# The end of a two-layer metaformer kernel: half-size PSUM tiles, wider bias passes, output biases on another engine, more repeated products

## The chip, the cores and the metric

The kernel runs on one core of a Trainium2 chip. A core has TensorE (PE; its weight loads are listed as PEld), VectorE (DVE), ScalarE (ACT), GpSimd (POOL) and SyncE (SP, which here issues most transfers), and 16 DMA engines that all queues share. Matrix products are written to PSUM, 128 partitions by eight banks of 512 fp32 values. The metric is the device time of one execution, the median of several runs, in microseconds (us). All data are fp32; each matrix product appears in the trace as two records.

## The reference

The input x is 16 samples of 128 channels by 32 x 32 positions (1024 tokens). Layer 0 adds linear attention and then a spectral convolution over the tokens. Layer 1 adds a residual block of two 3x3 convolutions to the normalised x, and then this mixture of 64 experts:

```python
def _L1_ffn_ref(x, gate_w, gate_b, weight1, weight2):
    logits = jnp.einsum('bsd,ed->bse', x, gate_w) + gate_b
    probs = jax.nn.softmax(logits, axis=1)            # over the 1024 tokens
    vals, idx = jax.lax.top_k(probs.transpose(0, 2, 1), K)    # K = 8
    ...
    pooled = jnp.einsum('bked,bke->bed', gathered, topv)
    h = jnp.concatenate([pooled.transpose(1, 0, 2), ones], axis=-1)
    h = jax.nn.gelu(jnp.einsum('ebd,edh->ebh', h, weight1), approximate=False)
    h = jnp.concatenate([h, ones], axis=-1)
    out = jnp.einsum('ebh,eho->ebo', h, weight2)
    out = out.transpose(1, 0, 2)
    weighted = jnp.einsum('beo,bke->bkeo', out, topv).reshape(Bn, K * E, O)
    outputs = jnp.zeros((Bn, Sn, O), dtype=x.dtype)
    outputs = outputs.at[jnp.arange(Bn)[:, None], flat_idx].add(weighted)
    return outputs
```

`x` here is the layer norm of each token over its channels. `weight1` has 129 rows of 512 per expert (the last is a bias), `weight2` 513 rows of 128 (the last is a bias). Each expert picks 8 tokens of a sample, pools them with their softmax weights, runs one small network on the pooled vector, and adds its output to the same tokens with the same weights.

## The kernel before

The change touches the end of layer 1. What comes ahead of it (layer 0, up to about 630 us) is unchanged.

**The convolution stage** takes the 16 samples one after another, overlapped. Every sample is a list of some fifty operations (`table`); a planner, given a duration and a due time for each, writes the order in which all engines issue them, and a few operations of the last samples are then moved by hand (`move`). The order is fixed: each engine executes its own instructions in that order. An operation is a method of `Routed`; sample 14 uses the subclass `Other`, sample 15, the last, uses `Final`. The last sample's part after its convolutions is, in this order:

- `last`: per half of the positions, DVE adds the residual and updates x, PE transposes four 128x128 blocks to tokens (`flip`), DVE takes statistics of the blocks (`count`);
- `stats2`, `root2`, `scales2`: the second half's statistics, then the scale and the shift of each token;
- `norm2`: four blocks are normalised on DVE and four on ACT;
- `channels`: PE transposes the tokens back, half by half, into `pu`, and DVE and ACT copy one half each into `tk`;
- `logits`: PE multiplies `tk` of samples 14 and 15 by the gate weights. `Final` does it twice, into two tiles, so that DVE (`replace`) and ACT (`exp`) have one each;
- `largest`: DVE finds the eight largest of each row (MAX8 on each half, then on the two results) and the bias of the exponential; `exp`: ACT, with the row sum; `replace`: DVE marks the eight largest (MATCH_REPLACE8);
- `gates`: DVE keeps the marked exponentials, PE transposes them, ACT and DVE copy one half each to `gtt`;
- `pool`, `pool_copy`, `pooled`, `pooled_copy`: PE pools the tokens by the gates, DVE scales, PE transposes, DVE copies to `pooled`.

PSUM has three one-bank slots (tag `cv`), two two-bank slots (tag `big`) and one more (tag `s`). A tile of tag `big` holds both halves of a sample. A tile that takes a slot over waits until the former tile's readers are done. `keep` issues products of the identity with itself into a tile of tag `cv`; nothing reads them.

**The experts** follow. They are taken in 16 groups of four. Group g: `hidden(g)` adds four products to biases that stand in PSUM already, and ACT applies GELU; `turn` transposes that (copied by DVE); `output` multiplies by the second weights (copied by DVE); `collect` transposes the result into `ot`. The loop runs them staggered: in iteration g PE issues `turn` of g-1, `hidden` of g, `collect` of g-2 and `output` of g-1. `biases(g)` writes the hidden biases of a pair of groups: for each of four experts and of two groups one product of a broadcast column of the identity (32 rows) with 32 rows of `b1`, into a 32-row strip of the group's PSUM bank. It runs before the loop for groups 0 and 1, into two `cv` slots, and in the loop at every even g, into a `big` slot.

The expert weights come as 32 pieces ("halves") of 1 MB. The first 15 are loaded before the loop; each later one is issued by SP when the product that used its place is done (`freed`), and after the weights ten loads of parked samples (`xb`). Once the expert outputs stand in `ob` (DVE: output times the sample's factor `rs`, plus the output bias, which ACT put there beforehand, L1951), the last stage (L1989) multiplies them by the gates of all samples, and DVE, or ACT with POOL, adds the products to x, which SP writes out, 512 KB a sample.

**Beside this**, at the head of the convolution stage (about 626 to 668 us) SP issues, in program order, the loads of samples 0 and 1, of the convolution weights `cw`, of `b1` (two loads) and of the output biases `b2` (two loads), and then those of samples 2 and up (x from `xd`, and `y` from `yd`).

Of the kernel before, what the change touches and what calls it, by code (L numbers as in the profile page):

```python
# [8 lines left out]
F32 = mybir.dt.float32  # L9
# [5 lines left out]
P = 128  # L15
# [54 lines left out]
def metaformer_kernel(ctx: ExitStack, tc: tile.TileContext, io: dict, out: bass.AP):  # L70
# [1029 lines left out]
    b1 = gpool.tile([E, HID], F32, name="b1")  # L1100
# [4 lines left out]
    with ExitStack() as c1:  # L1105
# [114 lines left out]
        idle = {(13, "turn"): 4, (13, "pooled"): 2, (15, "logits"): 2, (15, "turn"): 1}  # L1220
# [368 lines left out]

        class Other(Routed):  # L1590
# [12 lines left out]
        class Final(Routed):  # L1603
# [11 lines left out]
            def count(self, h):  # L1615
                for j in range(4 * h, 4 * h + 4, 2):
                    nc.vector.bn_stats(
                        self.bst[:, j : j + 2, :].rearrange("p j s -> p (j s)"),
                        self.pt[:, j : j + 2, :].rearrange("p j c -> p c j"),
                    )  # L1620

            def flip(self, dst, src, h):
                for j in range(4):
                    nc.tensor.transpose(dst[:, j, :], src[:, 4 * h + j], ident)

            def last(self):
                v = nc.vector
                self.pt = tokens(big())
                xj = self.x.rearrange("p (j c) -> p j c", c=P)
                for h in range(2):  # L1630
# [11 lines left out]
                    self.flip(self.pt[:, 4 * h : 4 * h + 4], xj, h)  # L1642
# [6 lines left out]
            def norm2(self, i):  # L1649
# [3 lines left out]
                r, nm = self.sts[:, 0, :], self.sts[:, 3, :]  # L1653
                for j in range(4):
                    nc.vector.tensor_scalar(
                        self.tt[:, j], self.pt[:, j], r[:, j : j + 1], nm[:, j : j + 1],
                        ALU.mult, ALU.add,
                    )
                normalize(self.tt, self.pt, r, nm, 4, NT)
# [8 lines left out]
            def logits(self):  # L1668
                super().logits()
                one = self.pl  # L1670
                super().logits()
                self.pl, self.pl2 = one, self.pl

            def exp(self):
                one, self.pl = self.pl, self.pl2
                super().exp()
                self.pl = one

            def largest(self):
                v = nc.vector  # L1680
                self.top = work.tile([P, TOPK], F32, name="top", tag="top")
                two = work.tile([P, 2 * TOPK], F32, name="two", tag="two", bufs=1)
                for h in range(2):
                    v.max(two[:, h * TOPK : (h + 1) * TOPK], self.pl[:, halves2[h]])
                v.max(self.top, two)
                self.ss = work.tile([P, 3], F32, name="sm", tag="sm")
                v.tensor_tensor(self.ss[:, 0:1], self.top[:, 0:1], gb, ALU.add)
                v.tensor_tensor(self.ss[:, 1:2], gb, self.ss[:, 0:1], ALU.subtract)

            def gates(self):  # L1690
                self.pg = tokens(big())
                self.gtt = work.tile([P, NT, P], F32, name="gtt", tag="tok", bufs=1)
                gj = self.gt.rearrange("p (j c) -> p j c", c=P)
                for h, copy in enumerate((nc.scalar.copy, nc.vector.tensor_copy)):
                    cs, js = halves2[h], slice(4 * h, 4 * h + 4)
# [3 lines left out]
                    self.flip(self.pg[:, js], gj, h)  # L1699
                    copy(self.gtt[:, js], self.pg[:, js])  # L1700
                nc.vector.reciprocal(rs[:, self.pr : self.pr + 1], self.ss[:, 2:3])
# [108 lines left out]

        def biases(g):

            for i in range(EG):
                for r in range(2):
                    rows = slice(r * E // 2, (r + 1) * E // 2)
                    at = r * E // 2 + g // 2 * EG + i
                    nc.tensor.matmul(
                        phs[g + r][i * CG : (i + 1) * CG, :],
                        ident[rows, at : at + 1].to_broadcast([E // 2, CG]), b1[rows, :],
                        start=True, stop=False, skip_group_check=True,  # L1820
                    )
# [22 lines left out]
        with tc.manual_schedule(engines=PINNED | {mybir.EngineType.SP}):  # L1844
# [4 lines left out]
            bs = w1[:, C, :].rearrange("(k r i) h -> r k i h", r=2, i=EG)  # L1849
            for r in range(2):  # L1850
                nc.sync.dma_start(b1[r * E // 2 : (r + 1) * E // 2, :], bs[r])
# [4 lines left out]
            for b, name in order:  # L1856
# [15 lines left out]
                if b == B - 1 and name == "logits":  # L1872
                    for g in range(2):
                        phs[g] = ps.tile([P, HID], F32, name="ph", tag="cv", bufs=3)
                    biases(0)
# [19 lines left out]
        def hidden(g):  # L1895
            w1t = halves[2 * g]
            if g % 2 == 0:
                if g:
# [262 lines left out]
```

## Time and profile before

| | us |
|---|---|
| median of 3 runs (lowest to highest) | 1220.72 (1220.01 to 1222.14) |
| the profiled execution's own time | 1224.1 |
| its span, first to last instruction | 1222.0 |
| busy: PE / DVE / ACT / POOL | 1145.7 / 943.2 / 727.2 / 604.7 |
| mean granted TensorE clock, share of full speed | 0.981 |
| first transposes of the last sample's tokens | 1112.75 |
| pooling of the last pair starts | 1130.08 |
| first products of the first expert group | 1133.24 |
| first final product | 1191.16 |
| first output issued | 1195.90 |

A line of the order of time gives start, duration, engine, source line, operation, written tile <- read tiles, shapes and count; the brackets hold how long the engine had stood idle and what ended that wait. A line of the stretches gives, for each engine, the busy time and the number of instructions, then the granted PE clock, the busy share of the DMA engines (it can read a few per cent over 1) and their rate. SPq lines are issues of transfers, and their time is that of issuing.

### The profile page before, as it was taken

Reading aid. Unit: us, or ns where it says so; the run is one execution under the profiler, and the core shown is the slowest. Engines: PE = TensorE matmul, PEld = TensorE weight load, DVE = VectorE, ACT = ScalarE, POOL = GpSimd, SP = SyncE. Lnnn points to the kernel's source line nnn. Section 1 sums busy time; section 2 is a strip of 40 time slices with the busy share of each in tenths; the row PEclk is TensorE's granted clock in tenths of the full one; section 3 lists DMA queues with packets and bytes.
Section 4 is the critical chain, followed back from the end, with each engine's and each line's share of the span. In section 5 each row is a group of like instructions: output and inputs, shape, how many; then the busy total and the mean of one; then the engine's idle time right before and its main releaser. Section 6 shows DMA issues by size and latency. Waiting matters only on the chain.

```text
span 1222.0 us, 34375 instructions
## 1 busy us (share of the span) xinstructions
PE 1145.7 (94%) x14322; PEld 941.2 (77%) x14322; DVE 943.2 (77%) x1953; ACT 727.2 (60%) x1447; POOL 604.7 (49%) x806
## 2 busy tenths in 40 slices
PE   6899999999998999999997899999999999998995
PEld 5667767787767999999996788888888888885452
DVE  6999999878655777777764689898888989877335
ACT  6777776878564777777752345555555555554211
POOL 2786436454557688888872434343333333231003
PEclk8999999999998999999998999999999999999997
DMA  7224463322234334444458311233233321416997
GB/s 285 87 91 173 159 208 117 104 87 86 71 123 146 97 134 142 141 135 140 141 175 265 99 52 53 86 103 120 80 119 116 104 87 70 173 35 238 369 408 312
DMA packets 91546, 175.13 MB, mean 143 GB/s; under 512 B 6016, under 2 KB 42112, under 8 KB 90752
## 3 DMA queue, kind: packets, MB, share of 16 engines
q1 hardware_dynamic: 88672, 168.95, 41.3%
q0 software_dynamic: 640, 2.49, 0.7%
q8 instruction: 112, 1.84, 0.6%
q10 hardware_dynamic: 2080, 1.51, 0.4%
q14 instruction: 42, 0.34, 0.1%
HBM read 110.28 MB, written 62.65 MB: 142 GB/s over the span
## 4 chain that ended last, share of the span: by engine, by line
PE 47%; DVE 27%; issue 11%; ACT 5%; DMA 5%; POOL 4%; SPq 0%; POOLq 0%; DVEq 0%; ACTq 0%
PE pcv L1211 10%; PE pg L987 9%; PE py L1011 9%; DVE bst L135 4%; PE big L573 3%; PE big L152 3%; PE big L172 3%; PE big L643 3%; DVE abss L1454 1%; DVE xp L1476 1%; PE big L534 1%; DVE xp L1338 1%; PE big L451 1%; DVE sts L128 1%; ACT tt L144 1%
## 5 line engine op out<-in xcount | busy, mean ns | idle before, releaser
L1211 PE MATMUL pcv<-v,cw 128*128 128x256 f32 x1152 | 259.9, 382 | 4.1 <-POOL v L1401 4.1
L1211 PEld LDWEIGHTS pcv<-v,cw 128*128 128x128 f32 x1152 | 215.9, 191 | 37.7 <-issue 4.9
L998 DVE COPY g<-pg 128x512 f32<-128x512 f32 x196 | 127.8, 683 | 70.6 <-PE pg L987 70.6
L1000 ACT COPY g<-pg 128x512 f32<-128x512 f32 x316 | 161.2, 606 | 30.1 <-PE pg L987 29.4
L987 PE MATMUL pg<-ph,mst 32*128 32x128 f32 x4096 | 139.3, 280 | 1.6 <-DVE x L650 0.9
L987 PEld LDWEIGHTS pg<-ph,mst 32*128 32x128 f32 x4096 | 126.5, 188 | 15.7 <-DVE g L998 8.2
L1011 PE MATMUL py<-g,v 128*32 128x128 f32 x4096 | 126.2, 276 | 4.3 <-POOL v L978 2.6
L1011 PEld LDWEIGHTS py<-g,v 128*32 128x32 f32 x4096 | 109.0, 111 | 12.5 <-POOL v L978 2.8
L144 ACT ACTIVATE tok<-tok,sts 128x128 f32<-128x128 f32 x256 | 101.9, 481 | 15.9 <-DVE sts L1288 13.6
L978 POOL TENSOR_TENSOR v<-xc 128x256 f32<-128x256 f32 x128 | 97.5, 785 | 15.8 <-DMA xc<-vd 15.5
L135 DVE BATCH_NORM_STATS2 bst<-big 128x6 f32<-128x256 f32 x252 | 89.6, 417 | 17.4 <-PE big L152 11.6
L643 PE MATMUL big<-u,mu 128*128 128x128 f32 (+4 forms) x384 | 86.2, 381 | 0.1
L1401 POOL TENSOR_TENSOR v<-abss 128x256 f32<-128x256 f32 x64 | 49.1, 787 | 68.1 <-DVE abss L1397 56.7
L1420 POOL TENSOR_TENSOR yo<-abss 128x256 f32<-128x256 f32 x32 | 23.5, 733 | 109.9 <-DVE abss L1416 109.9
L643 PEld LDWEIGHTS big<-u,mu 128*128 128x128 f32 x384 | 57.3, 191 | 23.8 <-issue 15.8
L573 PE MATMUL big<-wf,ub 128*128 128x256 f32 x256 | 65.1, 391 | 3.6 <-ACT ub L144 1.5
L476 POOL TENSOR_TENSOR ke<-ke,ks 128x1024 f32<-128x1024 f32 x16 | 30.6, 1915 | 72.4 <-DVE qs L484 42.7
L979 POOL TENSOR_SCALAR v<-v 128x256 f32<-128x256 f32 x64 | 55.2, 862 | 5.6
L573 PEld LDWEIGHTS big<-wf,ub 128*128 128x128 f32 x256 | 45.8, 192 | 15.4 <-ACT ub L144 7.9
L287 POOL TENSOR_TENSOR xf<-ab 128x256 f32<-128x256 f32 x34 | 25.2, 741 | 64.4 <-DVE ab L254 64.3
L144 ACT ACTIVATE tt<-tt,sts 128x128 f32<-128x128 f32 x120 | 47.8, 481 | 14.8 <-DVE sts L1288 13.1
L144 ACT ACTIVATE ub<-ub,sts 128x128 f32<-128x128 f32 x128 | 50.8, 479 | 8.9 <-DVE sts L566 8.9
(284 smaller groups left out, 2460.1 us busy)
## 6 DMA issues: line engine op xcount, KB each, us to landing
we<-in_weight SPq DMA_DIRECT2D x31, 1024.0 KB, 10.4
xc<-vd SPq DMA_DIRECT2D x64, 256.0 KB, 3.0
yd<-ys SPq DMA_DIRECT2D x32, 512.0 KB, 3.6
vd<-xf SPq DMA_DIRECT2D x15, 1024.0 KB, 5.1
y<-yd SPq DMA_DIRECT2D x15, 896.0 KB, 6.1
x<-in_x SPq DMA_DIRECT2D x16, 512.0 KB, 4.8
mi<-in_M_phi SPq DMA_DIRECT2D x16, 512.0 KB, 4.5
xd<-x SPq DMA_DIRECT2D x15, 512.0 KB, 3.0
```

The costliest lines, as they stand in the source:

```text
L135: nc.vector.bn_stats(bst[:, j : j + 2, :].rearrange("p j s -> p (j s)"), src[:, j : j + 2, :].rearrange("p j c -> p c j"),)
L144: nc.scalar.activation(dst[:, j, :], src[:, j, :], AF.Identity, bias=nm[:, j : j + 1], scale=r[:, j : j + 1],)
L573: nc.tensor.matmul(dst, self.ub[:, q, :], wf[:, q, :], start=True, stop=True)
L643: nc.tensor.matmul(self.pa[:, a:hi], mu[:, NF - 1 - si, tap, :], self.u[:, a - tap : hi - tap], start=(tap == 0), stop=(tap == KU - 1),)
L978: nc.gpsimd.tensor_tensor(vv[:, x, 1:, bs], e, o, op)
L979: nc.gpsimd.tensor_scalar(v[:, :, 0, bs], v[:, :, 2, bs], -1.0, None, ALU.mult)
L987: nc.tensor.matmul(pg[r][:, i], mst[rs, 4 * q + i, :], ph[rs, c, :], start=True, stop=True,)
L998: nc.vector.tensor_copy(dst, src)
L1000: nc.scalar.copy(dst, src)
L1011: nc.tensor.matmul(py[rows, x, kl, :], v[:, (x * NM + m) * JL + jl, 1 - ri : 3 - ri, :] .rearrange("p k b -> p (k b)"), g[:, ((x * 2 + ri) ...
L1211: nc.tensor.matmul(pc[:, i], wt[:, dy, k, :], v[:, k, dy * WT : dy * WT + HT], start=(dy == 0), stop=(dy == 2),)
L1401: nc.gpsimd.tensor_tensor(v[:, k, WT : WT + HT], self.ab[:, 0], self.ab[:, 1], op)
```

## The change

It does the following:

- In the last sample every two-bank tile of the tokens, of one set of logits and of the transposed gates becomes two one-bank tiles (`quarter()`, tag `cv`). The order of normalisation in `norm2` is turned round: ACT's half is issued first.
- One of the two sets of logits is computed half by half; each half's MAX8 follows its products, the exponential reads these halves in two instructions with a sum each, and a DVE addition joins the sums. `replace` reads the other set.
- In `gates` both gate products and transposes are issued before the two copies.
- `biases` does four groups in a pass: `b1` takes 128 partitions (16 rows of each 32 hold biases; a POOL memset clears the rest), is loaded in four pieces, and a pass has 16 products on 32x32 tiles of the array, into four banks. The first pass moves from behind `logits` to behind `gates`; the others run at g = 4, 8 and 12.
- The output biases move from ACT, ahead of the loop, to DVE inside it, one pair per iteration from g = 3 to 10.
- `keep` gets two more products after the logits, one less after the gates, and one in each of four places at the end of the expert stage.

```diff
-    b1 = gpool.tile([E, HID], F32, name="b1")
+    b1 = gpool.tile([P, HID], F32, name="b1")
+    nc.gpsimd.memset(b1, 0.0)
...
-        idle = {(13, "turn"): 4, (13, "pooled"): 2, (15, "logits"): 2, (15, "turn"): 1}
+        idle = {(13, "turn"): 4, (13, "pooled"): 2, (15, "logits"): 4}
...
+        def quarter():
+            return ps.tile([P, 4, P], F32, name="pq", tag="cv", bufs=3)
...
             def last(self):
                 v = nc.vector
-                self.pt = tokens(big())
+                self.half = []
...
                     if h:
                         self.count(0)
-                    self.flip(self.pt[:, 4 * h : 4 * h + 4], xj, h)
+                    self.half.append(quarter())
+                    self.flip(self.half[h], xj, h)
...
+                normalize(self.tt[:, 4:], self.half[1], r[:, 4:], nm[:, 4:], 0, 4)
                 for j in range(4):
                     nc.vector.tensor_scalar(
-                        self.tt[:, j], self.pt[:, j], r[:, j : j + 1], nm[:, j : j + 1],
+                        self.tt[:, j], self.half[0][:, j], r[:, j : j + 1], nm[:, j : j + 1],
                         ALU.mult, ALU.add,
                     )
-                normalize(self.tt, self.pt, r, nm, 4, NT)
...
             def logits(self):
+                self.two = work.tile([P, 2 * TOPK], F32, name="two", tag="two", bufs=1)
+                self.lg = []
+                for h in range(2):
+                    pl = quarter()
+                    self.lg.append(pl.rearrange("p j c -> p (j c)"))
+                    for jj in range(2):
+                        nc.tensor.matmul(
+                            self.lg[h][jj * E : (jj + 1) * E, :], gw,
+                            tks[self.b - 1 + jj][:, halves2[h]],
+                            start=True, stop=True, skip_group_check=True,
+                        )
+                    nc.vector.max(self.two[:, h * TOPK : (h + 1) * TOPK], self.lg[h])
                 super().logits()
-                one = self.pl
-                super().logits()
-                self.pl, self.pl2 = one, self.pl
...
+            def exp(self):
+                self.gt = work.tile([P, N], F32, name="eg", tag="eg", bufs=1)
+                for h in range(2):
+                    nc.scalar.activation(
+                        self.gt[:, halves2[h]], self.lg[h], AF.Exp, bias=self.ss[:, 1:2],
+                        accum_out=self.ss[:, 2 + h : 3 + h],
+                    )
...
-                for h, copy in enumerate((nc.scalar.copy, nc.vector.tensor_copy)):
-                    cs, js = halves2[h], slice(4 * h, 4 * h + 4)
+                pg = []
+                for h in range(2):
+                    cs = halves2[h]
                     nc.vector.scalar_tensor_tensor(
                         self.gt[:, cs], self.lr[:, cs], LOW, self.gt[:, cs], ALU.is_le, ALU.mult
                     )
-                    self.flip(self.pg[:, js], gj, h)
-                    copy(self.gtt[:, js], self.pg[:, js])
-                nc.vector.reciprocal(rs[:, self.pr : self.pr + 1], self.ss[:, 2:3])
+                    pg.append(quarter())
+                    self.flip(pg[h], gj, h)
+                for h, copy in enumerate((nc.scalar.copy, nc.vector.tensor_copy)):
+                    copy(self.gtt[:, 4 * h : 4 * h + 4], pg[h])
+                total = self.ss[:, 2:3]
+                nc.vector.tensor_tensor(total, total, self.ss[:, 3:4], ALU.add)
+                nc.vector.reciprocal(rs[:, self.pr : self.pr + 1], total)
...
+        BG, BR = 4, P // 4
+
         def biases(g):
+            for k in range(0, BG, 2):
+                two = ps.tile([P, 2, HID], F32, name="ph", tag="big", bufs=2)
+                phs[g + k], phs[g + k + 1] = two[:, 0], two[:, 1]
             for i in range(EG):
-                for r in range(2):
-                    rows = slice(r * E // 2, (r + 1) * E // 2)
-                    at = r * E // 2 + g // 2 * EG + i
+                for r in range(BG):
+                    rows = slice(r * BR, (r + 1) * BR)
+                    at = r * BR + g // BG * EG + i
                     nc.tensor.matmul(
                         phs[g + r][i * CG : (i + 1) * CG, :],
-                        ident[rows, at : at + 1].to_broadcast([E // 2, CG]), b1[rows, :],
+                        ident[rows, at : at + 1].to_broadcast([BR, CG]), b1[rows, :],
                         start=True, stop=False, skip_group_check=True,
+                        tile_position=(r * BR, i * CG),
                     )
...
-            bs = w1[:, C, :].rearrange("(k r i) h -> r k i h", r=2, i=EG)
-            for r in range(2):
-                nc.sync.dma_start(b1[r * E // 2 : (r + 1) * E // 2, :], bs[r])
+            bs = w1[:, C, :].rearrange("(k r i) h -> r k i h", r=BG, i=EG)
+            for r in range(BG):
+                nc.sync.dma_start(b1[r * BR : r * BR + E // BG, :], bs[r])
...
-                if b == B - 1 and name == "logits":
-                    for g in range(2):
-                        phs[g] = ps.tile([P, HID], F32, name="ph", tag="cv", bufs=3)
+                if b == B - 1 and name == "turn":
                     biases(0)
...
-            if g % 2 == 0:
-                if g:
-                    two = ps.tile([P, 2, HID], F32, name="ph", tag="big", bufs=2)
-                    phs[g], phs[g + 1] = two[:, 0], two[:, 1]
-                    biases(g)
+            if g and g % BG == 0:
+                biases(g)
...
-            for q in range(NPAIR):
-                nc.scalar.activation(ob[:, q], b2, AF.Identity, scale=rs[:, q : q + 1])
             for g in range(ng + 1):
...
                 if g > 1:
                     collect(g - 2, og.pop(g - 2))
+                if 2 < g < NPAIR + 3:
+                    q = g - 3
+                    nc.vector.tensor_scalar(ob[:, q], b2, rs[:, q : q + 1], None, ALU.mult)
                 if g:
+                    keep(ps, "cv", g == ng)
                     og[g - 1] = output(g - 1, ht)
                     freed(2 * g - 1)
+            keep(ps, "cv", 1)
             collect(ng - 1, og.pop(ng - 1))
+            keep(ps, "cv", 1)
...
+            keep(ps, "cv", 1)
             for q in range(NPAIR):
                 nc.vector.scalar_tensor_tensor(
```

More of the change, by code (lines that the diff above doesn't have):

```diff
@@ L1618, in count @@
                         self.bst[:, j : j + 2, :].rearrange("p j s -> p (j s)"),
-                        self.pt[:, j : j + 2, :].rearrange("p j c -> p c j"),
+                        self.half[h][:, j - 4 * h : j - 4 * h + 2, :].rearrange("p j c -> p c j"),
                     )
@@ L1668, in logits @@
             def logits(self):
-                super().logits()
-                one = self.pl
-                super().logits()
-                self.pl, self.pl2 = one, self.pl
[L1674 to L1677, printed above, removed]
+                self.two = work.tile([P, 2 * TOPK], F32, name="two", tag="two", bufs=1)
[10 more added lines that the diff above has]
+                    nc.vector.max(self.two[:, h * TOPK : (h + 1) * TOPK], self.lg[h])
+                super().logits()
             def largest(self):
@@ L1681, in largest @@
                 self.top = work.tile([P, TOPK], F32, name="top", tag="top")
[L1682 to L1686, printed above, removed]
+                v.max(self.top, self.two)
+                self.ss = work.tile([P, 4], F32, name="sm", tag="sl", bufs=1)
                 v.tensor_tensor(self.ss[:, 0:1], self.top[:, 0:1], gb, ALU.add)
                 v.tensor_tensor(self.ss[:, 1:2], gb, self.ss[:, 0:1], ALU.subtract)
+            def exp(self):
[5 more added lines that the diff above has]
+                    )
             def gates(self):
-                self.pg = tokens(big())
                 self.gtt = work.tile([P, NT, P], F32, name="gtt", tag="tok", bufs=1)
                 gj = self.gt.rearrange("p (j c) -> p j c", c=P)
-                for h, copy in enumerate((nc.scalar.copy, nc.vector.tensor_copy)):
-                    cs, js = halves2[h], slice(4 * h, 4 * h + 4)
+                pg = []
+                for h in range(2):
+                    cs = halves2[h]
                     nc.vector.scalar_tensor_tensor(
```

## The prediction

> **What bounds the kernel now.** I read the page first, then the last 110 us in stretches, the order of time of the same part, and the transfers. Page and stretches:
>
> ```profile
> span 1222.0 us, 34375 instructions
> PE 1145.7 (94%) x14322; PEld 941.2 (77%) x14322; DVE 943.2 (77%) x1953; ACT 727.2 (60%) x1447; POOL 604.7 (49%) x806
> core 0: us, PE busy (x) PEld busy (x) DVE busy (x) ACT busy (x) POOL busy (x), PEclk, DMA share, GB/s
> 1134.00:1194.00 60.00, 56.99 (x840) 29.35 (x838) 22.21 (x56) 9.56 (x16) 0.00 (x0) 0.98 1.04 398
> 1192.00:1204.00 12.00, 11.60 (x39) 5.76 (x40) 7.74 (x12) 2.02 (x2) 3.39 (x2) 0.72 0.53 213
> 1204.00:1220.00 16.00, 6.09 (x26) 3.11 (x22) 7.44 (x7) 2.02 (x2) 6.01 (x3) 0.76 1.03 419
> ```
>
> PE is the bound of the whole, but the change touches the last sample and what follows it, and there two things run at their limit together: PE without a gap, and the DMA engines at a share of 1.03 to 1.04. From 1134 to 1194 they stream expert weights and parked samples; from 1204 to 1220 outputs at 419 GB/s. Only 1192 to 1204 leaves them half idle. So my question for each edit is whether it moves the start of that stream or fills that hole; PE time saved elsewhere is not yet kernel time. The order of time shows the edited places:
>
> ```profile
> 1114.26 0.75 DVE L1617 BATCH_NORM_STATS2 bst<-big 128x6 f32<-128x256 f32 x2
> 1115.06 0.65 PE L1624 MATMUL big<-ident,xp 128*128 128x128 f32 x4 [1.68 <-DVE bst L1617]
> 1119.47 1.50 ACT L144 ACTIVATE tt<-big,sts 128x128 f32<-128x128 f32 x4 [1.48 <-DVE tt L1655]
> 1121.29 3.65 PE L1518 MATMUL big<-tk,gw 128*64 128x512 f32 x16
> 1125.19 1.21 DVE L1539 MATCH_REPLACE8 lr<-top,big 128x1024 f32<-128x1024 f32 x1
> 1129.06 0.66 PE L1624 MATMUL big<-ident,eg 128*128 128x128 f32 x4 [1.14 <-ACT gtt L1700]
> 1130.08 1.97 PE L1565 MATMUL pp<-tt,gtt 128*64 128x128 f32 x32
> ...
> 1152.06 1.09 PE L1817 MATMUL ph<-b,ident 32*32 32x512 f32 x16
> 1153.08 1.07 PE L1905 MATMUL ph<-we,pooled 128*32 128x512 f32 x8
> ...
> 1191.16 1.50 PE L1989 MATMUL pfy<-gt,ob 64*128 64x512 f32 x2 [0.45 <-DVE ob L1971]
> ```
>
> The three bracketed waits are the reader's: each names an instruction that works on the other half of the same two-bank PSUM tile.
>
> **The change, part by part.** The profiled execution took 1224.1 us, span 1222.0; the median shown is 1220.72, 3.4 below. I sum against the profiled one and carry the difference to the median.
>
> *Half tiles for the tokens* (`last`, `norm2`). The second half's transposes wait for the statistics of the first (end 1114.26 + 0.75 = 1115.01), though their input, the DVE update of x, ends at 1114.34. With a tile per half they start at 1114.40: -0.66 down to the scales. ACT's normalisation of the other half no longer waits for DVE's four (1.48 us) and runs beside them. Then the logits wait for DVE's copy of tk instead of ACT's half: 4 DVE normalisations, the last transpose (0.33), the copy (0.69), so 1121.29 becomes 1119.95. Together -1.34. The tiles come from three one-bank slots shared with the convolution, `pu`, the logits and the repeated products. If `pu` gets the slot that DVE still reads, its four transposes queue behind the fourth normalisation, +0.35; if not, 0. I take 0: a third slot is free.
>
> *Logits by half.* The maxima move ahead, but the replacement now reads the second set of products, which ends 3.65 after the start of the first. It waited 3.90 after that start; now 3.65 + 0.06 + 0.08 (value load) = 3.79. The exponentials, two of some 0.6 with two accumulator reads of 0.2 (the single one took 1.11), end inside the replacement's 1.21, so the gates follow the replacement by 0.04, not 0.12. Together -0.19.
>
> *Gates, output biases, first bias pass.* The second half's transposes wait 1.14 us for ACT's copy, which itself stood behind two `ob` activations (1127.85, 0.69). With a tile per half and `ob` on DVE they follow the gates (two DVE operations, 1126.52 to 1127.81) directly. But the first bias pass, which ran for nothing at 1124.87 beside the replacement, now stands on PE between these transposes and pooling. Before: pooling starts 2.27 after the gates. After: 0.05 + four issues of 0.11 + the pass 1.1 = 1.59, about when DVE's copy of the half is done (0.05 + 0.65 + 0.04 + 0.69). -0.68. The eight `ob` operations go into the loop, one per group, where DVE is busy 3.8 of 10 us: nothing; uncovered they would be 8 x 0.3.
>
> Front: -1.34 - 0.19 - 0.68 = **-2.2**. Everything behind pooling, the issue of the weight loads among it, comes that much earlier. Late next: pooling itself.
>
> *Bias passes in the loop.* Now at g = 2, 4, ... 14, seven of 1.02 (1152.06 to 1153.08). After: at 4, 8, 12, three passes of 16 tiles instead of 8. No row shows four row groups at once. Nearest row: this pass, where 16 records of 0.6 us fit in 1.09, so they overlap; with 16 more records staggered alike I take 1.1. Bounds: 1.02, and 4.4 if each row group needed a whole pass. PE: 3 x 1.1 - 7 x 1.02 = -3.8. Cover: the weights. The last two halves land at 1167.0 + 13.6 = 1180.6 and 1169.6 + 13.5 = 1183.1 and are used at 1184.90 and 1187.44, 4.3 later; 0.5 of that is left. A stall there only delays PE towards a stream that is the bound.
>
> The first final product thus moves by -6.0, from 1191.16 to 1185.2. The parked samples' loads, DMA-bound, end only 2.2 earlier: 1194 to 1192.
>
> *Repeated products.* Four more sit in PE's waits of 0.36 to 0.68 us before output, collect, the last transposes and the final products. One is two records of 0.215, 0.43. Where the wait is 0.36 (1189.62) it may cost 0.1: nothing. The four after the logits (1.7 us from 1123.4 on) end before the gates' transposes. Their purpose must be the clock:
>
> ```profile
> 1190.00:1192.00 2.00, 1.55 (x9) 0.77 (x7) 1.24 (x5) 0.00 (x0) 0.00 (x0) 0.94 1.03 420
> 1194.00:1196.00 2.00, 2.00 (x8) 0.98 (x6) 0.69 (x1) 0.00 (x0) 0.00 (x0) 0.50 0.20 80
> 1198.00:1200.00 2.00, 2.00 (x10) 1.14 (x9) 1.87 (x3) 0.48 (x1) 0.00 (x0) 0.85 0.82 319
> ```
>
> It fell to 0.50 although no gap ahead was over 0.7 us, while the transposes were thin. [...]
>
> *The end.* At full clock the first output leaves 3.7 after the first final product, at 1188.9: DVE still has to finish `ob` (2.2), PE the next products (0.86 + 0.16), DVE one addition (0.69). By 1192 there are 1 MB of outputs waiting, and DVE (4 x 0.69 + 10 x 1.22 = 15 us for 8.4 MB) stays ahead of 419 GB/s (20.0 us). So the hole closes: 12 us at 213 instead of 419 GB/s are 12 x 206/419 = **-5.9**. Bounds: 0, and -5.9; nearest is full, since the last additions are 8 us ahead of the DMA.
>
> *`b1` on 128 partitions, early.* POOL gets a memset; nearest row: 1.05 us for 128x1154, so 0.5, near 629 us before the folding of a chunk that SP writes out at 634.6 (0 to +0.5; I take +0.2, since the DMA is saturated behind it). SP issues four loads instead of two (1.03 each):
>
> ```profile
> 650.41 1.21 SPq L1848 DMA_DIRECT2D cw<-cwd  x2
> 651.66 2.06 SPq L1851 DMA_DIRECT2D b<-in_weight  x2
> 658.49 0.33 SPq L1231 DMA_DIRECT2D xp<-xd  x1
> 659.19 3.10 SPq L1234 DMA_DIRECT2D y<-yd  x2
> ```
>
> The issue at 658.49 falls on the landing of the load eight places before it (649.13 + 9.3), that at 661.69 on cw's (650.41 + 11.3): eight transfers are out at most. Two more shift sample 2's y to cw's second landing, 665.4, 6.2 later. PE stood 4.06 us on that y before 678.73. Price: between 0 (the DMA share from 663 to 674 is 1.04 and the same bytes stand ahead) and +6.2. Nearest: the saturated stretch; I take +0.3.
>
> Sum: -2.2 - 5.9 + 0.5 = -7.6: span 1214.4, profiled 1216.5, median **1213.1**.
>
> **Rivals.**
> - *The clock falls all the same.* Then outputs leave as now, 4.7 and more after the first final product, and the one behind POOL 11.9 after (1203.03), at 1197. The first 1.5 MB are gone by 1195.7; with some 1.5 from issue to data the DMA idles 2.8. Sum -4.8, 1215.9. For it: the fall now; against: 1.7 us more products in 4 us.
> - *Sample 2's y comes late.* +6.2 at most, middle 3: -4.6, worst -1.7 (1219.0). For it: the landings; against: the saturated DMA.
> - *The hole belongs to the profiled execution.* The runs are 3.4 shorter; were it all there, -7.6 + 3.4 = -4.2, 1216.5. Nothing tells where they are shorter.
> - *Four row groups do not overlap* (the other side). One pass of p: final products move by (3p - 7.14) + (-2.2 + p - 1.1) = 4p - 10.4; the end then stands 3.7 + 1.5 + 20.0 + 1.9 = 27.1 behind them, 30.8 now (first output, its latency, the bytes, the last landing). So it is slower from 4p - 10.4 = 3.7 on, p = 3.5; at 4.4, +3.5 + 0.5 = 1224.7. Against: two groups overlap fully at 1152.06, as do the halves of the final products.
> - *The waits stay* (slots collide, and the stream is as late as now): some -1, 1219.7, no change.
>
> **How the numbers follow.** 0.2% (2.4 us) is what a measurement can tell from none. Chances: forecast 0.57, clock 0.13, late y 0.11 (a third of it within 0.2%), profile's hole 0.08, rows 0.07, waits stay 0.04. Faster 0.57 + 0.13 + 0.07 + 0.08 = 0.85; same 0.04 + 0.04 = 0.08; slower 0.07. The forecast's own range is 1211 (stream fuller at its start, tail with no hole) to 1215.5. For 8 in 10: up to the late y's middle and the clock, 1217.8; below, 1210.8.
>
> **What would show it.** Right: ACT's four normalisations beside DVE's; `gates`' second transposes without a wait on ACT; bias rows x32 of about 1.1; clock 1.00 from 1184 on; DMA share near 1.03 without a hole from pooling to the end. Wrong: sample 2's y landing after 676, PE waiting for weights by more than 1 us in the loop, bias rows over 1.5, a hole between the last load and the outputs.

## The result, and the profile after

The changed kernel takes **1216.11 us** in the median (1214.04 to 1218.45, seven executions), the kernel before 1220.01 beside it (1218.09 to 1222.14, seven): 3.9 us less by the medians; over all fast executions the ratio is 0.9963 with a 95% interval of 0.9946 to 0.9981, which is 4.5 us (2.3 to 6.6) faster. With more executions of both later it was 1219.04 against 1222.35, 0.9974 (0.9960 to 0.9989). The forecast was 1213.1, -7.6 us: the direction and the range (1210.8 to 1217.8) hold, the size does not.

The two profiled executions alone would have hidden that: their spans are 1222.0 and 1214.1, and -7.9 looks like the forecast. The page and the stretches after:

```profile
span 1214.1 us, 34399 instructions
PE 1140.5 (94%) x14332; PEld 941.2 (78%) x14332; DVE 945.3 (78%) x1962; ACT 725.2 (60%) x1441; POOL 605.8 (50%) x807
core 0: us, PE busy (x) PEld busy (x) DVE busy (x) ACT busy (x) POOL busy (x), PEclk, DMA share, GB/s
1126.00:1150.00 24.00, 22.42 (x366) 12.44 (x345) 8.73 (x26) 4.90 (x8) 0.00 (x0) 1.00 1.02 381
1150.00:1175.00 25.00, 25.00 (x412) 13.29 (x415) 10.48 (x28) 4.79 (x8) 0.00 (x0) 1.00 1.05 403
1188.00:1192.00 4.00, 4.00 (x19) 2.32 (x17) 3.51 (x6) 1.01 (x1) 1.03 (x1) 1.00 1.02 410
1192.00:1196.00 4.00, 4.00 (x20) 2.38 (x18) 3.49 (x4) 1.41 (x2) 3.64 (x2) 1.00 0.99 398
1196.00:1200.00 4.00, 4.00 (x20) 2.62 (x17) 3.90 (x4) 1.17 (x2) 2.36 (x1) 1.00 0.97 388
1204.00:1208.00 4.00, 0.00 (x0) 0.00 (x0) 0.00 (x0) 0.00 (x0) 0.00 (x0) 0.50 1.02 418
```

The hole ahead of the outputs is closed: in these stretches, from pooling into the outputs, the DMA share stays at 0.97 or more, and the clock is 1.00 until PE has no more work. The order of time shows the edited places:

```profile
1112.80 0.63 PE L1629 MATMUL pq<-ident,xp 128*128 128x128 f32 x4 [1.11 <-DVE xp L1642]
1115.72 1.51 ACT L144 ACTIVATE tt<-pq,sts 128x128 f32<-128x128 f32 x4
1115.80 1.36 DVE L1662 TENSOR_SCALAR tt<-pq,sts 128x128 f32<-128x128 f32 x4
1117.91 2.35 PE L1681 MATMUL pq<-tk,gw 128*64 128x512 f32 x8
1122.09 1.21 DVE L1540 MATCH_REPLACE8 lr<-top,big 128x1024 f32<-128x1024 f32 x1
1124.14 1.25 PE L1629 MATMUL pq<-ident,eg 128*128 128x128 f32 x8 [0.24 <-DVE eg L1711]
1125.32 1.14 PE L1841 MATMUL ph<-b,ident 32*32 32x512 f32 x32
1126.39 1.97 PE L1566 MATMUL pp<-tt,gtt 128*64 128x128 f32 x32
...
1178.07 1.08 PE L1950 MATMUL peo<-we,ht 128*32 128x128 f32 x32 [0.62 <-DMA we<-in_weight]
...
1184.42 1.09 PE L2014 MATMUL pfy<-gt,ob 64*128 64x512 f32 x2
```

The three waits for the other half of a tile are gone; DVE and ACT normalise side by side; four row groups of biases take 1.14 us where two took 1.09; and near the end of the loop PE now waits 0.62 us for expert weights.

To compare profiles of executions that differ ahead of the edits, I count from one point of the program, the first addition that `last` makes on DVE (1110.77 before, 1109.07 after). Of the -7.9, -1.7 lies ahead of that point (-0.3 of it close to it, in both pairs of profiles), and -6.2 behind it. The table holds the profiles of all kernels but the last three, in us from that point. "Idle" is the time in which the DMA engines did nothing, as a mean over the 16 (worked out from their packets), from 30 us behind the first hidden product on; "trailing" is the time from when fewer than half of them were busy on average, for good, to the end of the span (both are good to 0.1 or 0.2 us); "fetch" tells whether a 16 KB transfer of instructions ran inside the outputs.

| kernel | first hidden product | first final product | first output | idle | fetch | trailing | end |
|---|---|---|---|---|---|---|---|
| before | 22.5 | 80.4 | 85.1 | 5.9 | no | 1.9 | 111.2 |
| before, second profile | 22.5 | 80.4 | 84.2 | 3.7 | no | 1.9 | 108.4 |
| after | 20.5 | 75.4 | 79.0 | 0.5 | yes | 3.2 | 105.1 |
| after, second profile | 20.5 | 75.7 | 79.3 | 0.4 | yes | 3.2 | 105.4 |
| after, no added products at the end | 20.5 | 75.1 | 79.0 | 1.1 | no | 1.9 | 104.9 |
| before, added products alone | 22.7 | 80.7 | 84.3 | 4.2 | yes | 3.7 | 110.5 |
| after, shorter program | 20.5 | 75.5 | 79.2 | 0.3 | no | 3.6 | 105.3 |
| before, longer program | 22.5 | 80.4 | 84.2 | 2.5 | yes | 3.4 | 109.9 |
| after, whole tiles as before | 23.6 | 77.7 | 80.4 | 0.2 | yes | 2.9 | 106.2 |
| after, bias passes of two groups | 20.6 | 78.6 | 81.3 | 1.5 | yes | 2.7 | 106.0 |
| before, wide bias passes alone | 24.2 | 78.4 | 81.1 | 0.3 | no | 2.9 | 107.1 |

### The profile page after: what moved, and what is told of

Read it like the earlier page. It is cut to its first block, busy times and chain, and to the rows that moved or that the text cites. A ratio compares the mean times of both kernels' runs of the same rounds, so it can differ in the third digit from the quotient of the medians.

```text
span 1214.1 us, 34399 instructions
## 1 busy us (share of the span) xinstructions
PE 1140.5 (94%) x14332; PEld 941.2 (78%) x14332; DVE 945.3 (78%) x1962; ACT 725.2 (60%) x1441; POOL 605.8 (50%) x807
## 5 line engine op out<-in xcount | busy, mean ns | idle before, releaser
L643 PEld LDWEIGHTS big<-u,mu 128*128 128x128 f32 x384 | 57.4, 191 | 23.6 <-issue 16.0
```

The lines of the kernel that those rows point to most:

```text
L643: nc.tensor.matmul(self.pa[:, a:hi], mu[:, NF - 1 - si, tap, :], self.u[:, a - tap : hi - tap], start=(tap == 0), stop=(tap == KU - 1),)
```

## The experiments

Theory: the edits of the last sample's chain, of the bias passes and of the repeated products close a hole in the transfers, and some 6 us at the end are theirs. First rival: the hole of 5.9 us was that of one execution. Later rivals concern what still counts once the DMA engines never rest.

**The kernel before, again**

> The kernel before, unchanged, to see what one profiled execution of it has in common with another. Theory (the hole belongs to the kernel): its profile again shows the clock falling to 0.50 for about 6.8 us once PE reaches the last transposes and the first final products, and the DMA share near 0.5 for about 12 us between the last parked load and the stream of outputs; the time is that of before within 0.2%. Rival (the hole belongs to the one profiled execution): the clock stays at 1.00 there, the first output leaves about 3.7 us after the first final product instead of 4.7, and the thin stretch is 9 us or less. Either way, falls of the clock in the first 1100 us at other places than 157.5, 652.5 and 679.8 us would say that the earlier part of two profiles differs by chance.

1222.26 us against 1222.35, ratio 1.0002 (0.9986 to 1.0018). The stretches of its tail:

```profile
1188.00:1192.00 4.00, 2.55 (x44) 1.86 (x43) 1.42 (x4) 0.00 (x0) 0.00 (x0) 1.00 1.03 416
1192.00:1196.00 4.00, 2.78 (x12) 1.18 (x11) 2.30 (x9) 0.00 (x0) 0.00 (x0) 1.00 0.83 339
1196.00:1200.00 4.00, 4.00 (x18) 2.17 (x16) 3.57 (x5) 1.01 (x1) 0.51 (x1) 1.00 0.64 246
1200.00:1204.00 4.00, 4.00 (x21) 2.53 (x17) 3.45 (x3) 1.01 (x1) 4.00 (x2) 1.00 0.71 290
```

The clock did not fall here, and the hole is shallower: shares of 0.83, 0.64 and 0.71 where the first profile had 0.53 over the same stretch; 3.7 us of idle engines, not 5.9. Counted from the common point the end comes 2.8 us earlier. So there is a hole in the kernel, and 2.2 us of what I priced belonged to one execution, in which the clock fell for 6.83 us. The rival was right, as far as two profiles of the kernel can tell.

**The changed kernel, again**

> The changed kernel, unchanged, for a second profile and a narrower interval. Theory (the three edits at the end are worth what the two profiles show from 1100 us on, -7.9 + 1.4 = -6.5 us): faster than before by 5.5 to 7 us, and from pooling to the last output the DMA share again has no stretch under 0.9. Rival (before usually has a smaller hole): faster by 3 to 4.5 us with the same tail.

1219.04 against 1222.35: -3.3 us (1.3 to 4.9 by the interval). The rival's 3 to 4.5, and the second pair of profiles agrees: 108.4 to 105.4.

**The added products taken out of the changed kernel**

```diff
-                    keep(ps, "cv", g == ng)
                     og[g - 1] = output(g - 1, ht)
...
-            keep(ps, "cv", 1)
             collect(ng - 1, og.pop(ng - 1))
-            keep(ps, "cv", 1)
...
-            keep(ps, "cv", 1)
             for q in range(NPAIR):
```

> The changed kernel without its four added products in the last waits. Theory (PE that works thinly lets the clock fall, and half speed in the first final products opens a hole ahead of the outputs): the clock falls to 0.50 between about 1184 and 1192 us, the first output leaves about 1 us later (1189 instead of 1188), what POOL adds about 3 us later, and the DMA engines run thin for some 2.8 us: about 1219, 2.8 us above the changed kernel. [...] Second rival (the clock falls, but the queue of outputs is long enough): clock at 0.50 and less than 1 us.

1218.14, ratio 0.9970 (0.9955 to 0.9986): no slower than the changed kernel's 1219.04. The stretches:

```profile
1184.00:1188.00 4.00, 2.78 (x14) 1.42 (x14) 2.16 (x8) 0.00 (x0) 0.00 (x0) 1.00 1.02 417
1188.00:1192.00 4.00, 4.00 (x14) 1.86 (x10) 2.61 (x5) 0.00 (x0) 0.00 (x0) 0.57 1.02 415
1192.00:1196.00 4.00, 4.00 (x22) 2.36 (x20) 3.15 (x3) 2.02 (x2) 2.35 (x2) 1.00 0.93 365
1196.00:1200.00 4.00, 4.00 (x19) 2.39 (x18) 3.90 (x5) 1.01 (x1) 3.48 (x3) 1.00 0.89 363
```

The clock did fall, for 3.41 us from 1188.0 on, but the DMA engines were busy with parked samples until then; the share drops only to 0.93 and 0.89, and the end is not later. The second rival was right in what it foresaw, no loss at the end; this fall was half as long as the 6.83 us of the first profile of before, and it came once the front and the loop had moved the outputs ahead. Not foreseen: without these products the trailing time is 1.9 instead of 3.2 us, while the idle time is 0.6 us longer. So the run changed two things at once, and the price of the fall by itself is not shown.

**The added products alone, on the kernel before** (the same four `keep` lines put in)

> The kernel before with the four products in the last waits alone. Theory (clock): it stays at 1.00 from the last transposes on, the first output leaves 3.7 us after the first final product instead of 4.7, POOL's first addition starts 6.5 us after it instead of 9.5, and the end comes about 3 us earlier than before, near 1217; the DMA share is still thin for some 8 us, since the first final product is as late as before. [...]

1223.35, ratio 1.0010 (0.9992 to 1.0029): no gain. The clock stayed at 1.00 and POOL's first addition came 6.5 us after the first final product, as the theory had it, but so it nearly does in the second profile of before, where the clock stayed up without them. And the trailing time is 3.7 us: in the last 1.9 us of the transfers one DMA engine alone was still busy (19 to 29 GB/s). In this profile and in the two of the changed kernel a 16 KB transfer of instructions ran on one DMA engine inside the outputs (for 1.68 us from 1196.79 in the first of the changed kernel); in the kernels without the products it did not. That became the next pair.

**A program 16 instructions shorter, and one 16 longer**

```diff
-            keep(ps, "cv", 26)
+            keep(ps, "cv", 22)
```

on the changed kernel, and 30 instead of 26 on the kernel before: the products at the start of the convolution stage, 500 us ahead of the edits.

> The changed kernel with 22 instead of 26 repeated products at its very start, so that PE's program is 16 instructions shorter up to the end, as it is without the four products of the last waits. In the profiles so far a transfer of 16 KB of instructions took 1.68 us on one DMA engine at 1196.79, in the middle of the outputs, in the two profiles of the changed kernel, and the last packets trailed: from the time when fewer than half of the DMA engines were busy to the end of the span 3.2 us passed, 1.9 us without the four products and without that transfer. Theory (the fetch of instructions delays one engine, and with no hole behind it to catch up in the delay lasts to the end): no fetch between 1185 and the last output, trailing time 1.9 us, the span 1.3 us shorter than that of the changed kernel counted from one point ahead of the edits; as a time about 1217.7 where the changed kernel takes 1219.0, which is less than the measurement tells. Rival (the trailing comes with the closed hole or the full clock): 3.2 us stay.

> The kernel before with 30 instead of 26 repeated products at its very start: PE's program is 16 instructions longer up to the end, as it is with the four products in the last waits, which are not in this kernel. Theory of the fetch: a transfer of 16 KB of instructions at about 1203 to 1205, within the outputs, and a trailing time of 3.2 to 3.7 us instead of the 1.9 of before. Rival: no such transfer or no effect, trailing 1.9. On the clock: if it falls in the tail in some executions only, this profile is one more look; by the theory of thin PE work it falls to 0.50 between 1184 and 1200 more often than not, by chance alone there is no telling.

On the kernel before it came out as expected. From 1200 to 1222 us, rate of the transfers in 40 slices and what ran; the second profile of before first, then the longer program:

```profile
GB/s 149 432 410 112 52 417 417 417 424 410 424 402 439 402 439 402 440 410 417 425 410 395 432 410 424 410 432 417 417 439 395 447 402 432 194 0 0 0 0 0
q1 hardware_dynamic: 2072, 7.42, 82.7%
```

```profile
GB/s 432 320 15 231 432 402 439 402 439 387 402 402 432 402 432 410 432 395 425 402 432 402 432 410 425 432 402 432 410 432 425 432 395 45 22 30 0 0 0 0
q8 instruction: 1, 0.02, 0.4%
```

With the fetch (1204.44, 1.42 us on one engine) the last slices are 45, 22 and 30 GB/s instead of a sharp end, where all 16 engines had moved some 420, or 26 each: it looks as if one engine was late by what the fetch took. End 109.9 instead of 108.4, +1.5, in one pair of profiles (the first profile of before ended at 111.2 without such a fetch); as a time 1222.20 against 1222.30, so no difference can be told.

On the changed kernel the theory fell: the fetch was gone from the outputs, yet the trailing time was 3.6 us.

```profile
GB/s 454 380 454 380 454 402 439 410 432 410 432 402 417 417 417 425 417 425 417 425 410 425 410 425 410 402 171 164 112 37 0 0 0 15 0 0 15 0 0 0
```

Several engines end late here. What fits all the profiles: trailing is 1.9 us where the engines had at least a microsecond of idle time behind the last fetch (before twice, after without the products), and 2.7 to 3.7 us where a fetch came behind the hole or there was no hole. Delays of single engines, caught up in a hole and kept without one, would fit that; only the fetch by itself was tried, so no run shows it. The time is 1217.91 against 1222.30, 0.9965 (0.9951 to 0.9979), the changed kernel's.

**The last sample's tiles as before, the rest changed**

```diff
-                    self.half.append(quarter())
-                    self.flip(self.half[h], xj, h)
+                    self.flip(self.pt[:, 4 * h : 4 * h + 4], xj, h)
```

and so on in `Final`: all its methods as in the kernel before.

> The changed kernel with the last sample's chain as before (one two-bank tile for tokens, logits and gates, with its waits), the wide bias passes, the output biases on VectorE and the added products kept. Theory (the transfers bound the end from pooling on, so what comes earlier there comes earlier at the end): the first product of the hidden layer comes 1.5 to 2.0 us later than in the changed kernel, counted from one point ahead of the edits, and the end as much: 1.5 to 2.0 us above it. Rival (the front is hidden behind weights that are still under way): hidden layer later, end the same within 0.3 us.

1221.12, ratio 0.9980 (0.9963 to 0.9998). The first hidden product is 3.1 us later than in the changed kernel, more than expected, since the first bias pass now follows a longer chain; the end is 0.7 to 1.1 us later by the profiles, 0.7 to 2.1 us in time, against the changed kernel's ratios of 0.9974 and 0.9963 (less than the intervals tell apart). Half between theory and rival: from the common point to 5 us behind the first hidden product the DMA engines idle some 2.3 us more (5.3 against 2.8 and 3.0), and more than half of it is not seen at the end. Where that half went stays open.

**Bias passes of two groups, the rest changed**

```diff
-            if g and g % BG == 0:
-                biases(g)
+            if g % 2 == 0:
+                if g:
+                    two = ps.tile([P, 2, HID], F32, name="ph", tag="big", bufs=2)
+                    phs[g], phs[g + 1] = two[:, 0], two[:, 1]
+                    biases(g)
```

> The changed kernel with bias passes of two groups, eight of them, the first at the same place as in the changed kernel, and with the biases on 64 partitions in two loads. Theory (from pooling on the transfers are the bound, PE's time in the loop counts only as far as it delays the first output beyond the last parked load): the first final product comes 3.0 us later than in the changed kernel (seven passes of 1.02 instead of three of 1.14, less the wait for weights of 0.6 that goes), the DMA engines stand half idle for about 1 to 1.5 us, and the end comes 1 to 1.5 us later. Rival (each microsecond of PE's loop is one of the end): the end comes 3 us later.

1218.22, ratio 0.9963 (0.9948 to 0.9978): the same as with the wide passes. The first final product is 3.0 us later, as expected, the idle time 1.0 us longer, the end 0.6 to 1.0 us later by the profiles. PE's three microseconds in the loop are worth one at the end, or less.

**Wide bias passes alone, on the kernel before**

```diff
+                if b == B - 1 and name == "turn":
+                    biases(0)
...
+            if g and g % BG == 0:
+                biases(g)
```

The body of `biases`, the tile `b1` and its loads are as in the change.

> The kernel before with the wide bias passes alone (four groups, the first behind the gates' transposes, biases on 128 partitions in four loads). PE in the loop: seven passes of 1.02 become three of 1.14, -3.7; ahead of pooling the pass costs up to 1.1. Theory (idle time of the transfers is what counts): first hidden product 0.5 to 1.1 us later, first final product 2.6 to 3.2 us earlier, and the span counted from one point ahead of the edits 1.5 to 2.5 us shorter, since the hole ahead of the outputs shrinks by as much as the first output comes earlier and no transfer starts sooner. Rival (the end follows PE alone): 2.6 to 3.2 us shorter. Second rival (stream starts later by the pass, and the hole takes the rest): under 1 us. The clock in the tail is one more look at how often it falls without the added products.

1219.02 against 1222.20, ratio 0.9978 (0.9965 to 0.9991), 2.7 us (1.1 to 4.3). The pass on the path costs more than thought (first hidden product +1.7), the first final product is 2.0 us earlier, and the end, counted from the common point, 1.3: a little less than the theory's 1.5 to 2.5, and the interval of the time holds the theory and the first rival both. Either half of the change alone closes most of the hole: the idle time is 0.3 us with the passes alone, 1.5 with all but the passes and 0.4 to 0.5 with both, from 3.7. The ends are 107.1, 106.0 and 105.1 to 105.4, from 108.4: the halves gain 1.3 and 2.4, together 3.0 to 3.4 instead of 3.7. Both draw on the same idle time of the DMA engines, which would explain that it is less than the sum; a difference of 0.3 to 0.7 us between single profiles does not show it.

**The loads of the biases, and a larger load beside them**

The loads of `b1` and `b2` were moved from ahead of sample 2's y to behind sample 4's:

```diff
                     if b > 1:
                         load(b)
+                    if b == 4:
+                        bs = w1[:, C, :].rearrange("(k r i) h -> r k i h", r=BG, i=EG)
+                        for r in range(BG):
+                            nc.sync.dma_start(b1[r * BR : r * BR + E // BG, :], bs[r])
...
```

> The changed kernel with the six small loads of biases (four b1, two b2) moved from in front of sample 2's y to behind sample 4's. It tests the step on the loads of b1. Theory (the transfers before sample 2's y are a saturated stream, so places in the queue of outstanding loads cost nothing and only bytes count, 0.2 MB or 0.5 us): sample 2's y is issued some 3 us earlier than at 665.26, lands at most 0.5 us earlier, and from 620 us to 700 us the kernel gains 0.3 to 0.5 us. Rival (the place in the queue decides when y lands): y lands 3 us earlier and the kernel is 2 to 3 us faster than the changed kernel.

Then the second convolution's weights alone, and both:

```diff
-            for n in range(2):
-                nc.sync.dma_start(cw[n], cwd[n])
+            nc.sync.dma_start(cw[0], cwd[0])
...
+                    if b == 2:
+                        nc.sync.dma_start(cw[1], cwd[1])
```

> The changed kernel with the second convolution's weights (1.15 MB) loaded behind sample 2's y instead of in front of it, all else the same. In the profiles POOL stands 10 us for that y and PE 3.0 us for POOL behind it. Theory (the saturated stream decides, bytes ahead count): y lands up to 1.15 MB / 415 GB/s = 2.8 us earlier, PE's 3.0 us shrink to under 1, and the kernel is 1.5 to 2.8 us faster than the changed kernel, some 0.5% faster than before. Rival (the second convolution's weights, or the first of sample 1's steps, are late next): PE waits for them instead, gain under 0.5 us.

> The changed kernel with both moves: the second convolution's weights behind sample 2's y, the bias loads behind sample 4's. Theory: the gains add, 2 to 3.3 us under the changed kernel, near 1215 where before takes 1222. Rival: another wait takes their place and it is under 0.5 us.

| kernel | median | ratio to before (1222.20) | 95% interval |
|---|---|---|---|
| bias loads later | 1213.39 | 0.9934 | 0.9914 to 0.9955 |
| `cw[1]` later | 1211.73 | 0.9921 | 0.9901 to 0.9940 |
| both | 1212.86 | 0.9922 | 0.9902 to 0.9942 |

Each beats both kernels, and they do not add. The changed kernel did not run beside them: by its own ratios, 0.9963 and 0.9974, the bias loads gain 3.5 to 4.9 us over it and the other two 5.0 to 6.5 (in five or six executions each), more than the theories and the rivals said. PE's waits and two stretches around it, in the changed kernel and then with `cw[1]` later:

```profile
PE pcv L1212 <- POOL v L1402: 3.0, 1, 3.0
655.00:670.00 15.00, 11.72 (x75) 10.07 (x74) 8.70 (x20) 4.92 (x12) 3.46 (x5) 0.89 0.84 265
670.00:685.00 15.00, 11.73 (x55) 9.77 (x54) 7.31 (x18) 6.93 (x14) 5.03 (x7) 0.89 0.62 153
```

```profile
PE pcv L1212 <- POOL v L1402: 0.7, 1, 0.7
655.00:670.00 15.00, 11.03 (x75) 9.34 (x74) 10.24 (x23) 4.41 (x11) 4.53 (x7) 0.96 0.91 235
670.00:685.00 15.00, 13.89 (x84) 12.05 (x85) 10.04 (x23) 8.88 (x17) 5.93 (x8) 1.00 0.69 211
```

POOL took its operations in the program's order; the one that needs sample 2's y stands ahead of the one that PE waits for (673.24 and 676.70 in the changed kernel). This is the one that needs y, in the changed kernel, with `cw[1]` later and with both moves:

```profile
673.24 0.78 POOL L1248 TENSOR_TENSOR z<-y 128x256 f32<-128x256 f32 x1 [9.91 <-DMA y<-yd]
```

```profile
671.77 0.94 POOL L1248 TENSOR_TENSOR z<-y 128x256 f32<-128x256 f32 x1 [7.36 <-PE big L172]
```

```profile
672.38 0.95 POOL L1248 TENSOR_TENSOR z<-y 128x256 f32<-128x256 f32 x1 [7.12 <-DMA y<-yd]
```

The second line names PE, and so does the profile of the bias loads alone. But y had landed only 0.02 us ahead of that product of PE there (671.61 and 671.63), and 0.08 us ahead in the other, and the profile puts a wait down to whatever came last. In all fourteen profiles POOL starts 0.16 to 0.25 us after the second load of sample 2's y has landed, so y is what it waits for in all of them, and the moves bring y forward: counted from POOL's start on sample 0's y it lands after 19.1 to 19.7 us in these three kernels, and after 20.9 to 23.2 in the eleven others (22.6 and 21.4 in the changed kernel). POOL starts on it after 19.2 to 19.9 us, and after 21.2 to 23.3.

The rest of the gain is the clock: in all eleven profiles where PE stood 2.3 to 4.1 us here, the clock fell to 0.50 within 1.1 us of the end of this wait, for 3.41 or 6.83 us; in the three where it stood 0.4 to 1.9, it did not. From POOL's start on sample 2's y to the common point the three kernels take 434.4 us, the changed kernel 435.8 and 435.9, and the one profile with 6.83 us at half clock 437.5. Both parts together, from sample 0's y to the common point, are 453.6 to 454.3 us against 457.6 and 458.7 of the changed kernel: 3.2 to 5.1 us.

For the bias loads alone the rival was right that y would land earlier by more than their bytes: 0.2 MB, or 0.5 us, is too little for the 1.7 to 2.9 us by which it did. Its y was issued at 656.44 instead of 665.26. But the time of issue does not decide alone: with both moves y was issued as early, at 656.45, with fewer bytes ahead of it, and landed no sooner. Of the 16 parts in which its second load reports the landing, 15 had come after 17.2 us and the last one after 19.3, and POOL waited for that. So both moves together gave no more than one because of one late part; what held it up, and what POOL would have waited for next, stays open.

## Why the prediction was right or wrong

- **What bounds the end.** Right. From 30 us behind the first hidden product to the last outputs the transfers stand idle for only 0.4 to 0.5 us, and PE's time counts only as far as it moves their start or fills the hole: 3.0 us more of it in the loop made the end 0.6 to 1.0 us later.
- **Half tiles for the tokens, -1.34:** from the common point to the logits -1.68. **Logits by half, -0.19:** +0.28; their 16 records took some 4.1 us instead of 3.65, so the replacement came 4.18 after their start. **Gates, -0.68:** -0.59; pooling starts 1.71 after the gates (forecast 1.59); the move of the output biases, which is part of this term, was not tried by itself. Together -2.0 for the forecast -2.2.
- **Bias passes, 1.1 us each, -3.8 in the loop:** the passes took 1.14 for 32 records of 0.6, so row groups overlap and the rival on the other side falls. From the first hidden to the first final product it came to -3.0 (first pair) and -2.7 (second). I left 0.5 us of slack for the weights; there was none, and PE waited 0.62.
- **Repeated products:** that they hold the full clock, on which the -5.9 stands, was my estimate, and no run shows it: the clock fell in the tail in 2 of 5 profiles without the four at the end and in none of 9 with them, which fits but is too little; and in four of the nine the clock fell for 3.41 us somewhat earlier, between 1110 and 1130 us. From 1180 us up to the fall in the tail of the first profile of before no gap of PE was above 0.68 us. What failed is the price: my rival "the clock falls all the same" gave the fall 2.8 us of idle transfers, with 1.5 us from issue to data, where the first output's data moved 0.84 us after its issue at 1195.90. Without the products, in a fall half as long, the idle time was 0.6 us longer and the end no later, with a shorter trail.
- **The end, -5.9: the step that failed.** "So the hole closes" is right, 0.4 to 0.5 us of idle is left. But the term was sized from one profile in which the clock had fallen. In the second, 3.7 us were idle; so the term is 3.2. I named this as a rival ("the hole belongs to the profiled execution", -4.2, 1216.5) and gave it 0.08, on the ground that nothing tells where the median runs are shorter. The profile held a hint: 6.83 us at 0.50 with the first final products in it. The measured 1216.11 and -3.3 to -4.5 us are that rival's. That the range held owes something to luck: its upper end was set by a late y and by the clock, and neither came.
- **Not in the sum:** the last transfers trail by 1.3 us more (3.2 against 1.9); no run shows why. Front -2.0, hole -3.2, trailing +1.3 make -3.9; the ends of the profiles without a fall differ by -3.0 to -3.4, and where the other 0.5 to 0.9 us went stays open.
- **`b1` on 128 partitions, +0.5:** nothing. Sample 2's y is issued at 665.26, as forecast, but POOL reaches it 22.3 us after sample 0's in the mean of the five profiles with two loads and 21.9 in the six with four at that place. I also took the 4.06 us wait for PE's own on y; it is POOL that waits for y and PE for POOL.
- **Rivals.** "Late y", "four row groups" and "the waits stay" fall by the readings above.

## What to carry to other kernels

A term worked out from one profile carries that execution's accidents; before a hole is priced, look whether the clock fell in it, and take a second profile. Where transfers run without a pause from some point to the end, count the idle time of the DMA engines rather than PE's: parts that save the same idle time need not add (here 1.3 and 2.4 us, together 3.0 to 3.4), and look at how the last transfers trail (3.2 us in the changed kernel, 1.9 before). When a wait is put down to an engine, look how long before it the transfer landed that the same instruction needs. And a load that several engines wait for in order should be issued ahead of the larger or the smaller ones that are needed later; here that was worth about as much as the whole change, or more (3.5 to 6.5 us against 3.3 to 4.5).

## What the runs showed of the hardware that was not expected

- The falls of the clock ahead of PE's last product lasted 3.41, 6.83 or 10.24 us (157.54, 389.65 and 14.18 us in the first profile of before), and they come and go in unchanged code: near 157 us in 9 of 14 profiles, which are 1.6 us longer from 156 to 170 us than the other five. At sample 2's y the clock fell behind waits of PE of 2.3 us (wide passes alone) and 2.4 us (the changed kernel, second profile).
- A 16 KB fetch of instructions took 0.9 to 1.7 us on one DMA engine, and where one fell inside the last outputs of the kernel before, the end came 1.5 us later in the one pair of profiles that tried it; the times do not tell it, and on the changed kernel the trail stayed without the fetch.
